# PSUM banks by longest idle time, odd rows' statistics in other steps, edge corrections on GpSimd, and the A sums in two halves

## The chip, the cores and the metric

The kernel runs on one core of a Trainium2 chip. The core has five engines that run side by side and meet only through semaphores: TensorE (PE in the profile) multiplies matrices into PSUM, VectorE (DVE) and ScalarE (ACT) work elementwise and can read PSUM, GpSimd (POOL) works elementwise on SBUF, and SyncE (SP) issues all the DMAs of this kernel. PSUM has eight banks of 128 x 512 fp32 values; SBUF is the working memory. The metric is the device time of one execution in microseconds (us), as a median over runs.

## The reference

A batch of 16 images of 256 channels by 64 x 64 pixels goes through two residual layers, everything in fp32:

```python
x = x + _L0_conv_ref(_gn(x), ...)   # layer 0
x = x + _L1_conv_ref(_gn(x), ...)   # layer 1

# _L0_conv_ref
pooled = x.mean(axis=(2, 3))
angles = jnp.tanh(relu(pooled @ ap_w1.T + ap_b1) @ ap_w2.T + ap_b2) * (math.pi / 4)
w = rotate(base_kernel, angles)                 # bilinear, per image and group
feat = conv3x3(x, w, groups=B * 8)
return feat * sigmoid(relu(pooled @ meta_w1.T + ...) @ meta_w2.T + ...)

# _L1_conv_ref, N = 4096 tokens of 256 channels, 8 heads of 32
q, k = focus(xt @ Wq.T + bq), focus(k)          # relu, / scale, cubed, old norm kept
z = 1.0 / (einsum(q, k.sum(axis=1)) + 1e-06)
out = einsum(q, einsum(k, v)) * z + depthwise5x5(v)
return out @ Wproj.T + bproj
```

`_gn` is a group norm with 32 groups. So every image needs the statistics of its input before the first convolution, and those of the first layer's output before the second layer's products.

## The kernel before

**Stages.** Image b passes through a key loop (16 steps n, `key_step`), a short passage `between`, and an attention loop (17 steps p, `attention_step`). During b's attention loop the 3x3 convolution of image b+1 is run piece by piece, and the input statistics of image b+2 are taken. During b's key loop the rotated weights of b+1 are prepared (`prepare`, a generator that is advanced twice a step). The main loops stand in `tc.manual_schedule()`: every engine gets its instructions in the order in which the Python code records them, and executes them in that order. An instruction that waits holds up all that follow on its engine.

**Convolution of b+1.** A half image u (0, 1) of two strips is convolved in parts. P multiplies odd input rows, A and B use sums of two neighbouring rows that GpSimd makes (`add_rows`, four instructions L384, one for each group j, into `arena`). `PARTS` gives the step at whose end a part is multiplied (`convolve`, four PSUM banks `pc` at once, L405): A in step 2, P in 3, B in 4 for u=0, and 9, 10, 11 for u=1. The next step evicts (`evict`): A first by ScalarE (L432), P by ScalarE (L428) and VectorE (L434), B by VectorE (L430). `SUMS` gives the steps in which the sums are made: 1 and 3, 8 and 10. Four DMAs for each j bring the rows into `arena` (`load_rows`, L371 to L376); for u=0 they are issued in the last key steps (j=3, 2) and just ahead of `between` (j=1, 0). The sums' region overlaps the value buffers `vbuf` 0 to 3 of the key loop.

**Settling.** After P the even rows (s=0) of an output are done, after B the odd ones (s=1). `settle` adds a correction to the first and last column of 8 rows (L443) and takes the statistics of the 512 values (L444). `SETTLES` gives step, (u, s, early q, late q), q running over four outputs. From step 14 on, `norm1` turns these statistics into coefficients: bn_aggr (L190), matmul pm (L196), four small VectorE instructions (L197 to L200), matmul pv (L203), a power on GpSimd (L206), the scaling of the key weights (L531) and matmul pbkv (L538).

**Statistics of b+2.** `more_stats` takes one chunk of 512 columns (L118) and issues the load of the next one into the same buffer `xs` (L109). `STATS` gives the step.

**One attention step.** In this order: ratio (L572, L573, VectorE) and root (L576, GpSimd) for f[p-1]; eviction of output 0; `add_up` (L756: adds py of p-3 to x) and `store` of the result (L762); `turn` (transposes pt, L698) with ScalarE's copy to qT (L703); eviction 1; `cube` of f[p] (GpSimd, L567); query products pq of p+1 (L683) and `query_bias` (VectorE, L557, L558); early settles; a step of `norm1`; evictions 2 and 3 with `turn_back` (transposes po of o, L734, copied by ScalarE, L736) between them; late settles; squares on ScalarE (L564); `attend` (matmuls pn, L715; VectorE zz and o, L717 to L724; GpSimd adds fm to o, L726); `project` (py, L744); sums, loads of value blocks (`load_blocks`, vh, L643, as many as `BLOCKS` says) and of rows; the convolution part; `more_stats`. In step 9 the second half of the depthwise products pd is computed.

**Query weights.** In the key loop `fold_load(b, "q")` loads them, `fold_scale` at n=5 scales them (L531), and `fold_shift` at n=6 multiplies them with the means (pbq, L538) and corrects the bias (L540).

**Banks.** `bank(name)` takes a 128 x 512 tile from a pool of six PSUM buffers with one tag, and the pool chooses the buffer. The remaining two banks hold pkv and pn.

Of the kernel before, what the change touches and what calls it, by code (L numbers as in the profile page):

```python
# [9 lines left out]
F32 = mybir.dt.float32  # L10
# [3 lines left out]
PSUM = bass.MemoryType.PSUM  # L14

P = 128
# [5 lines left out]
CH = 512  # L22
# [2 lines left out]
ROWS = CH // W  # L25


STRIP = 2 * ROWS
PAIRS = ROWS
LATE, LEAD = 3, 2  # L30
# [1 line left out]

PARTS = {2: (0, "A"), 3: (0, "P"), 4: (0, "B"), 9: (1, "A"), 10: (1, "P"), 11: (1, "B")}

SUMS = {1: (0, "A"), 3: (0, "B"), 8: (1, "A"), 10: (1, "B")}

SETTLES = {4: (0, 0, (0, 1), (2, 3)), 5: (0, 1, (0, 1), ()), 6: (0, 1, (2, 3), ()),
           11: (1, 0, (0, 1), (2, 3)), 12: (1, 1, (0, 1), ()), 13: (1, 1, (2, 3), ())}
SECOND, ONES_AT, FOLD_AT = 9, 13, 14

BLOCKS = {1: 2, 2: 4, 3: 3, 4: 4, 5: 1, 6: 1, 7: 1}
PIECES = {5: (0, 5), 6: (5, 10), 7: (10, 16)}
KEY_PIECES = {10: (0, 2), 11: (2, 4), 12: (4, 6), 13: (6, 8)}

STATS = {1: (0,), 2: (1,), 3: (2,), 7: (3,), 8: (4,), 9: (5, 6), 10: (7,)}
RAW = (STRIP + 2) * W
BR, BC = 8, 4
NR, NJ = H // BR, W // BC
# [15 lines left out]
def conv_attention(ctx: ExitStack, tc: tile.TileContext, x, consts, kw, b1, w2, b2, b2r,  # L64
                   wkv, wq, brow, srow, wp, bp, dwb, band, out):
    nc = tc.nc
    B = x.shape[0]

    def pool(name, bufs, **kw):
        return ctx.enter_context(tc.tile_pool(name=name, bufs=bufs, **kw))  # L70
# [7 lines left out]
    sp = pool("stats", 2)  # L78
    wtp = pool("wt", 1)
    dcp = pool("scratch1", 1, space=bass.MemoryType.DRAM)  # L80
    ps = pool("ps", 6, space=PSUM)
    psk = pool("psk", 1, space=PSUM)

    def const(name, shape, src=None):
# [2 lines left out]
            nc.sync.dma_start(t, src)  # L87
        return t

    def bank(name):  # L90
        return ps.tile([P, CH], F32, tag="bank", name=name)

    def halves(a):
        return a.rearrange("(t p) n -> p t n", p=P)
# [90 lines left out]
    def gn_coefs(st, b, which):  # L185


        mv = sp.tile([P, 2, 2], F32, tag="mv", name=f"mv{which}_{b}")
        for t in range(2):
            nc.vector.bn_aggr(mv[:, t, :], st[:, t])  # L190
        yield
        mean, var = mv[:, :, 0], mv[:, :, 1]
        co = sp.tile([P, 5, 2], F32, tag=f"co{which}", name=f"co{which}_{b}")
        a, pooled, d, v, m = (co[:, k, :] for k in range(5))
        pm = bank(f"pm{which}_{b}")[:, 0:2]
        nc.tensor.matmul(pm, lhsT=g8, rhs=mean, start=True, stop=True)  # L196
        nc.vector.tensor_copy(m, pm)  # L197
        nc.vector.tensor_sub(d, mean, m)
        nc.vector.tensor_mul(v, d, d)
        nc.vector.tensor_add(v, v, var)  # L200
        yield
        pv = bank(f"pv{which}_{b}")[:, 0:2]
        nc.tensor.matmul(pv, lhsT=g8, rhs=v, start=True, stop=True)  # L203
        vs = sp.tile([P, 2], F32, tag="vs", name=f"vs{which}_{b}")
        nc.vector.tensor_scalar(vs, pv, EPS_GN, None, ALU.add)
        nc.gpsimd.tensor_tensor(a, vs, mhalf, ALU.pow)  # L206
        yield
        if which == 0:
            nc.vector.tensor_mul(pooled, d, a)
        return a, pooled, m  # L210
# [7 lines left out]
    def prepare(b):  # L218
# [13 lines left out]
                                 start=t == 0, stop=t == 1)  # L232
        h = sp.tile([HID, 2], F32, tag="h", name=f"h_{b}")
        nc.vector.tensor_add(h, ph, b1_t)
        nc.vector.tensor_scalar(h, h, 0.0, None, ALU.max)
        yield
        pa = bank(f"pa_{b}")[:, 0:2 + 2 * HD]
# [10 lines left out]
        nc.vector.tensor_add(z, pa[:, 0:2], b2_t)  # L248
        mod = r_mod
        nc.vector.tensor_add(mod, pmod, b2r_t)  # L250

        nc.scalar.activation(mod, mod, AF.Tanh, scale=0.5)
        cs = sp.tile([P, 3, 2], F32, tag="cs", name=f"cs_{b}")
# [5 lines left out]
        pe = bank(f"pedge_{b}")[:, 0:NH]  # L259
        nc.tensor.matmul(pe, lhsT=sel, rhs=gm.rearrange("p t j -> p (t j)"), start=True, stop=True)  # L260
        nc.vector.tensor_copy(edge, pe)
        state[b]["edge"] = edge
        nc.vector.tensor_scalar(mod, mod, 0.5, 0.5, ALU.mult, ALU.add)
        yield
# [59 lines left out]
        def shifts(t):  # L324


            pb = bank(f"pbias_{b}_{t}")[:, 0:3]
            for j in range(4):
                for dx in range(3):
                    nc.tensor.matmul(pb[ts(j, HD), dx:dx + 1], lhsT=sums[t][:, dx, :], rhs=gm[:, t, j:j + 1],  # L330
                                     start=True, stop=True, tile_position=(0, HD * j))
            nc.vector.tensor_copy(shift[:, t, 0:3], pb)
            nc.vector.tensor_reduce(shift[:, t, 3:4], shift[:, t, 0:3], AX.X, ALU.add)
            nc.vector.tensor_scalar(shift[:, t, 3:4], shift[:, t, 3:4], -1.0, None, ALU.mult)

# [39 lines left out]
            else:  # L375
                nc.sync.dma_start(d, src[:, lo:hi])  # L376

    def add_rows(b, u, part):


        g, s = rows_of(b, u), sums_of(b, part)
        even, odd = (0, 1) if part == "A" else (2, 1)
        for j in range(4):
            nc.gpsimd.tensor_add(s[:, j], g[:, j, odd:odd + STRIP:2], g[:, j, even:even + STRIP - 1:2])  # L384

    def convolve(b, u, part):
# [32 lines left out]
    def evict(b, u, part, q):  # L419

        at, shift = (2 * u + q // 2, q % 2), state[b]["shift"][:, q % 2, 3:4]
        pc = state[b]["pc"][q].rearrange("p (r w) -> p r w", w=W)
        fresh = at not in state[b]["x"]
        if fresh:
            state[b]["x"][at] = xp.tile([P, 2 * CH], F32, tag="x", name=f"x_{b}_{at[0]}_{at[1]}")
        rows = rows_16(b, u, q)
        if part == "P":
            nc.scalar.activation(rows[:, 1], pc, AF.Identity, bias=shift, scale=-1.0)  # L428
        if part == "B":
            nc.vector.tensor_add(rows[:, 1], pc, rows[:, 1])  # L430
        elif fresh:
            nc.scalar.activation(rows[:, 0], pc, AF.Identity, bias=shift)  # L432
        else:
            nc.vector.tensor_add(rows[:, 0], pc, rows[:, 0])  # L434

    def settle(b, u, s, q):

        I, t = 2 * u + q // 2, q % 2
        if u == 0 and q == 0 and s == 0:
            state[b]["st1"] = sp.tile([P, 2, NCH, 6], F32, tag="st1", name=f"st1_{b}")  # L440
        rows, shift = rows_16(b, u, q)[:, s], state[b]["shift"]
        e = rows[:, :, 0:W:W - 1]
        nc.vector.tensor_add(e, e, shift[:, t, 0:3:2].unsqueeze(1).to_broadcast([P, PAIRS, 2]))  # L443
        nc.vector.bn_stats(state[b]["st1"][:, t, 2 * I + s, :], rows)  # L444

    load_kernels(0)
# [57 lines left out]
    for co in range(2):  # L504
        for t in range(2):
            nc.tensor.matmul(pb[:, co:co + 1], lhsT=wp_t[:, t, ts(co, P)], rhs=dwb_t[:, t:t + 1],
                             start=t == 0, stop=t == 1)
    nc.vector.tensor_add(bp_t, bp_t, pb)


    vpad = [dcp.tile([BC, H + 4, NJ, C], F32, tag=f"vpad{n}", name=f"vpad{n}") for n in range(2)]
# [21 lines left out]
    def fold_shift(b, name):  # L533
        w, br = state[b][name]
        n = br.shape[1]
        pb = bank(f"pb{name}_{b}")
        for t in range(2):
            nc.tensor.matmul(pb[:, 0:n], lhsT=state[b]["gn1"][1][:, t:t + 1].to_broadcast([P, P]), rhs=w[:, t, :],  # L538
                             start=t == 0, stop=t == 1)
        nc.vector.tensor_sub(br, br, pb[:, 0:n])  # L540

    def norm1(b):
        a, _, m = yield from gn_coefs(state[b]["st1"], b, 1)
# [48 lines left out]
    def key_bias(b, n, j):  # L592
        _, br = state[b]["kv"]
        f = state[b]["k"][n]
        pm = f["pm"][j]
        relu(f["r"][:, j:j + 1, :], pm[:, 0:C].unsqueeze(1), br[:, 0:C].unsqueeze(1))
        nc.vector.tensor_add(vbuf[n % NV][:, j, 0:HD, :].rearrange("p c h -> p (c h)"), pm[:, C:2 * C], br[:, C:2 * C])

    def key_store(b, n):
        for j in range(2):  # L600
# [47 lines left out]
    def depthwise(b, half, c):  # L648
# [7 lines left out]
        for k in range(4):  # L656
            for j in range(4):
# [6 lines left out]
                )  # L664
        nc.scalar.copy(fm[:, :, c * NH:(c + 4) * NH].rearrange("p T (k h) -> p k T h", k=4),
                       pd.rearrange("p k (T h) -> p k T h", h=NH))


    def blocked(b, m):
# [19 lines left out]
    def query_bias(b, m):  # L689
        f = state[b]["f"][m]  # L690
        relu(f["r"], f["pq"], state[b]["q"][1].unsqueeze(1).to_broadcast([P, 2, C]))

    def turn(b, m):

# [6 lines left out]
    def turned(b, m):  # L701
        qT = op.tile([P, 2, 2, P], F32, tag="qT", name=f"qT_{b}_{m}", bufs=1)
        nc.scalar.copy(qT, state[b]["pt"])  # L703
        state[b]["qT"] = qT

    def attend(b, m):
# [22 lines left out]
    def turn_back(b, m):  # L729

        po = bank(f"po_{b}_{m}").rearrange("p (t j n) -> p t j n", t=2, j=2)
        for j in range(2):
            for t in range(2):
                nc.tensor.transpose(po[:, t, j, :], state[b]["o"][j][:, ts(t, P)], ident)  # L734
        oT = op.tile([P, 2, 2 * P], F32, tag="oT", name=f"oT_{b}_{m}", bufs=1)
        nc.scalar.copy(oT.rearrange("p t (j n) -> p t j n", j=2), po)  # L736
        state[b]["oT"] = oT

    def project(b, m):
# [12 lines left out]
    def add_up(b, m):  # L752
        i, R = divmod(m, 2)
        for co in range(2):
            xt = chunk(b, i, co).rearrange("p (y R n) -> p R y n", y=BR, R=2)[:, R]
            nc.vector.scalar_tensor_tensor(xt, state[b]["py"][:, co], bp_t[:, co:co + 1], xt, ALU.add, ALU.add)  # L756

    def store(b, m):
        I, R = divmod(m, 4)
# [60 lines left out]
    def between(b, more):  # L820
# [25 lines left out]
        values(b, NP - 1)  # L846
        squares(f[0], 1)
        squares(f[1], 0)
        if more and b + 2 < B:
            load_stats(b + 2, 0)  # L850

    def attention_step(b, p, chain):
# [8 lines left out]
        if p - 1 < NP:  # L861
            ratio(f[p - 1], True)
            root(f[p - 1])
        if part:
            evict(b + 1, u, part, 0)
        if p >= 3:
            add_up(b, p - 3)
            store(b, p - 3)
        if p - 1 < NP:
            turn(b, p - 1)  # L870
            turned(b, p - 1)
# [70 lines left out]
    with tc.manual_schedule():  # L942
        fold_load(0, "q")
        made = iter(())
        for b in range(B):
            more = b + 1 < B
            state[b]["f"], state[b]["xq"] = {}, {}
            for n in range(0 if b == 0 else LEAD, NP):
# [13 lines left out]
                    fold_load(b, "q")  # L962
                if n == 5:
                    fold_scale(b, "q")
                if n == 6:
                    fold_shift(b, "q")
                if 7 <= n < 15:
                    load_blocks(b, 2 * n - 14)
# [97 lines left out]
```

## Time and profile before

| | |
|---|---|
| median of three runs | 3659.57 us (3655.64 to 3660.37) |
| profiled execution | 3660.74 us, its span 3659.0 us |
| granted TensorE clock | 0.994 of full speed, mean |
| one image, pbkv to pbkv, from the third on | 221.6 to 222.9 us |
| TENSOR_TENSOR x<-x,shift (L443) | 256 times, mean 263 ns |
| BATCH_NORM_STATS2 st<-x (L444) | 256 times, mean 694 ns |
| BATCH_NORM_STATS2 st<-xs (L118) | 256 times, mean 682 ns, 31.7 us of waits for DMA in 21 places |
| TENSOR_TENSOR arena<-arena (L384, GpSimd) | 244 times, mean 1279 ns |
| TENSOR_TENSOR arena<-arena,consts 128x32 (L316, GpSimd) | 32 times, mean 239 ns |

A line of the profile's waits reads: engine, what it was about to do and its line, then what it waited for, and the total in us, the number of waits and the longest. A line of the timeline reads: start and length in us, engine, line, operation, output<-inputs and their size, number of merged instructions, and in brackets the idle time ahead of it with what ended it. PE is TensorE's matmul, PEld its weight load; SPq is SyncE's issue of DMAs. Durations of matmuls are modelled ends of a pipeline, so neighbouring ones overlap.

### The profile page before, as it was taken

The numbers are of one execution on the slowest core, as the hardware profiler recorded it, in microseconds if no ns is written. First come the engines' busy times: TensorE is split into PE (matmuls) and PEld (weight loads), VectorE is DVE, ScalarE is ACT, GpSimd is POOL, SyncE is SP. The second block draws the span as 40 slices with busy tenths as digits, with TensorE's granted clock in tenths as the row PEclk, the third lists the DMA queues.
The fourth block names the chain that finished last, engine by engine and source line by source line (L and its number), as shares of the span: only waits on it lengthen the run. The fifth ranks groups of instructions, "written<-read, shape, count | busy, mean of one in ns | idle before, by whom it ended". The sixth has DMA issues, their size and how long they took to land. (4 is left out here: it accounts for less than half of the span.)

```text
span 3659.0 us, 109568 instructions
## 1 busy us (share of the span) xinstructions
PE 3425.6 (94%) x43496; PEld 2563.6 (70%) x43496; DVE 2541.2 (69%) x6883; ACT 2034.6 (56%) x6501; POOL 1980.4 (54%) x2298
## 2 busy tenths in 40 slices
PE   2899999999999999999999999999999999999999
PEld 1467777776777767776677777777777677767778
DVE  4667768676686767767677686776866677676656
ACT  2365655647556465654656556475564646546565
POOL 4255555556555465554655555565554655546545
PEclk9899999999999999999999999999999999999999
DMA  4353552625436253452635526354362534525242
GB/s 134 110 180 106 161 159 86 197 87 184 140 115 190 83 189 111 150 172 72 203 106 161 158 87 193 91 185 139 113 191 84 186 114 148 168 77 181 78 145 99
DMA packets 191172, 505.90 MB, mean 138 GB/s; under 512 B 30741, under 2 KB 103959, under 8 KB 178372
## 3 DMA queue, kind: packets, MB, share of 16 engines
q1 hardware_dynamic: 190660, 498.89, 42.8%
q8 instruction: 344, 5.64, 0.6%
q14 instruction: 168, 1.38, 0.1%
HBM read 363.24 MB, written 135.53 MB: 136 GB/s over the span
## 5 line engine op out<-in xcount | busy, mean ns | idle before, releaser
L588 PE MATMUL pk<-wkv,x 128*128 128x512 f32 x2048 | 951.5, 611 | 0.0
L726 POOL TENSOR_TENSOR o<-o,fm 128x256 f32<-128x256 f32 x512 | 364.8, 733 | 918.9 <-DVE o L724 704.7
L588 PEld LDWEIGHTS pk<-wkv,x 128*128 128x128 f32 x2048 | 617.6, 310 | 213.6 <-issue 6.5
L683 PE MATMUL pq<-wq,xq 128*128 128x256 f32 x2048 | 492.2, 383 | 21.7 <-DVE x L434 11.5
L744 PE MATMUL py<-oT,wp 128*128 128x256 f32 x2048 | 505.7, 390 | 0.8 <-ACT oT L736 0.7
L564 ACT ACTIVATE r_k<-rk 128x256 f32<-128x256 f32 x1024 | 416.3, 407 | 152.9 <-POOL rk L567 92.6
L564 ACT ACTIVATE r_q<-rq 128x256 f32<-128x256 f32 x1024 | 413.5, 408 | 138.5 <-POOL rq L567 135.9
L683 PEld LDWEIGHTS pq<-wq,xq 128*128 128x128 f32 x2048 | 369.9, 191 | 72.1 <-DVE x L434 15.3
L736 ACT COPY oT<-po 128x512 f32<-128x512 f32 x256 | 150.1, 586 | 469.5 <-PE po L734 469.1
L744 PEld LDWEIGHTS py<-oT,wp 128*128 128x128 f32 x2048 | 369.2, 189 | 51.4 <-issue 3.6
L567 POOL TENSOR_TENSOR rk<-r_k,rk 128x512 f32<-128x512 f32 x256 | 327.0, 1277 | 96.7 <-ACT r_k L564 94.1
L576 POOL TENSOR_TENSOR s_k<-s_k,phalf 128x2 f32<-128x2 f32 x256 | 176.8, 691 | 356.9 <-DVE s_k L573 345.5
L557 DVE TENSOR_TENSOR pq<-pq,bq 128x512 f32<-128x512 f32 x256 | 177.4, 693 | 272.7 <-PE pq L683 230.6
L608 ACT ACTIVATE rk<-rk,s_k 128x256 f32<-128x256 f32 x512 | 231.4, 499 | 213.7 <-POOL s_k L576 213.7
L567 POOL TENSOR_TENSOR rq<-r_q,rq 128x512 f32<-128x512 f32 x256 | 327.2, 1278 | 0.0
L384 POOL TENSOR_TENSOR arena<-arena 128x512 f32<-128x512 f32 x244 | 303.8, 1279 | 7.1 <-PE pc_0B L405 3.7
L557 DVE TENSOR_TENSOR pk<-pk,bkv 128x256 f32<-128x256 f32 x512 | 218.0, 426 | 121.7 <-PE pk L588 119.9
L703 ACT COPY qT<-pt 128x512 f32<-128x512 f32 x256 | 148.7, 581 | 261.9 <-PE pt L698 260.2
L715 PE MATMUL pn<-kvx,qT 128*128 128x132 f32 x2048 | 274.0, 277 | 0.0
L576 POOL TENSOR_TENSOR s_q<-s_q,phalf 128x2 f32<-128x2 f32 x256 | 179.3, 700 | 144.1 <-DVE s_q L573 140.4
L715 PEld LDWEIGHTS pn<-kvx,qT 128*128 128x128 f32 x2048 | 250.5, 190 | 3.7 <-ACT qT L703 3.1
L658 PE MATMUL pd<-vh,band 107*32 107x128 f32 x8192 | 236.3, 274 | 6.5 <-issue 4.5
(161 smaller groups left out, 5974.1 us busy)
## 6 DMA issues: line engine op xcount, KB each, us to landing
vh<-vpad SPq DMA_DIRECT2D x256, 384.0 KB
vh<-vpad SPq DMA_DIRECT2D x256, 360.0 KB
vpad<-arena SPq DMA_DIRECT2D x512, 128.0 KB
out<-x SPq DMA_DIRECT2D x128, 512.0 KB
xs<-in_x SPq DMA_DIRECT2D x224, 256.0 KB
arena<-in_x SPq DMA_DIRECT2D x248, 144.0 KB
arena<-in_x SPq DMA_DIRECT2D x248, 136.0 KB
xs<-in_x SPq DMA_DIRECT2D x16, 512.0 KB
```

Source lines behind the costliest of these rows:

```text
L384: nc.gpsimd.tensor_add(s[:, j], g[:, j, odd:odd + STRIP:2], g[:, j, even:even + STRIP - 1:2])
L557: nc.vector.tensor_add(pm, pm, bias)
L564: nc.scalar.activation(f["r2"][:, j, :], f["r"][:, j, :], AF.Square, accum_out=f["s"][:, k, j:j + 1])
L567: nc.gpsimd.tensor_mul(f["r"], f["r2"], f["r"])
L576: nc.gpsimd.tensor_tensor(f["s"][:, 3, :], f["s"][:, 2, :], phalf, ALU.pow)
L588: nc.tensor.matmul(pm, lhsT=chunk(b, n // 2, t)[:, T % BC:CH:BC], rhs=w[:, t, :], start=t == 0, stop=t == 1)
L608: nc.scalar.mul(f["r"][:, j, :], f["r"][:, j, :], f["s"][:, 3, j:j + 1])
L658: nc.tensor.matmul(pd[ts(j, HD), k, :].rearrange("p (R m h) -> p R m h", R=4, m=4), lhsT=band_t[:, c + k, :], rhs=vb[:, :, :, j, c + k, :] ...
L683: nc.tensor.matmul(pq[:, j, :], lhsT=xq[:, t, ts(j, P)], rhs=w[:, t, :], start=t == 0, stop=t == 1)
L715: nc.tensor.matmul(pn[:, :, 4 * hh:4 * hh + 4], lhsT=qT[:, hh, j, :], rhs=kvx[:, hh], start=True, stop=True)
L726: nc.gpsimd.tensor_add(o, o, fm[:, 2 * (m % NCH) + j, :])
L744: nc.tensor.matmul(py[:, co].rearrange("p y (J c) -> p J y c", c=BC), lhsT=wp_t[:, t, ts(co, P)], rhs=oT[:, t, :].rearrange("p (J y c) -> ...
```

## The change

`bank` now keeps a list of the free banks in the order in which the code gave them back (`leave`, called after the last reader of a tile has been recorded), and hands out the one that has been in the list longest; each bank is a tag of its own with one buffer. `leave` is recorded for every tile that `bank` gives. The tables `SUMS`, `SETTLES` and `STATS` are changed: the A sums of u=0 are made for j=0, 1 at the end of `between` and for j=2, 3 in step 1; odd rows are settled in steps 8, 9 and 13, 14 instead of 5, 6 and 12, 13; input statistics move among steps 2, 3, 7 and 8. The edge correction moves from VectorE to GpSimd. In `attention_step`, `add_up` and `store` come ahead of eviction 0. `fold_shift` of the query weights moves from n=6 to n=8.

```diff
-SUMS = {1: (0, "A"), 3: (0, "B"), 8: (1, "A"), 10: (1, "B")}
-
-SETTLES = {4: (0, 0, (0, 1), (2, 3)), 5: (0, 1, (0, 1), ()), 6: (0, 1, (2, 3), ()),
-           11: (1, 0, (0, 1), (2, 3)), 12: (1, 1, (0, 1), ()), 13: (1, 1, (2, 3), ())}
+SUMS = {1: (0, "A", (2, 3)), 3: (0, "B", range(4)), 8: (1, "A", range(4)), 10: (1, "B", range(4))}
+
+SETTLES = {4: (0, 0, (0, 1), (2, 3)), 8: (0, 1, (0,), ()), 9: (0, 1, (1, 2), (3,)),
+           11: (1, 0, (0, 1), (2, 3)), 13: (1, 1, (0, 1), ()), 14: (1, 1, (2, 3), ())}
...
-STATS = {1: (0,), 2: (1,), 3: (2,), 7: (3,), 8: (4,), 9: (5, 6), 10: (7,)}
+STATS = {1: (0,), 2: (1, 2), 3: (3,), 7: (4,), 9: (5, 6), 10: (7,)}
...
-    ps = pool("ps", 6, space=PSUM)
+    ps = pool("ps", 1, space=PSUM)
...
+    idle, held = [f"bank{k}" for k in range(BANKS)], {}
+
     def bank(name):
-        return ps.tile([P, CH], F32, tag="bank", name=name)
+        held[name] = idle.pop(0)
+        return ps.tile([P, CH], F32, tag=held[name], name=name)
+
+    def leave(name):
+        idle.append(held.pop(name))
...
-    def add_rows(b, u, part):
+    def add_rows(b, u, part, js=range(4)):
...
-        for j in range(4):
+        for j in js:
             nc.gpsimd.tensor_add(s[:, j], g[:, j, odd:odd + STRIP:2], g[:, j, even:even + STRIP - 1:2])
...
         e = rows[:, :, 0:W:W - 1]
-        nc.vector.tensor_add(e, e, shift[:, t, 0:3:2].unsqueeze(1).to_broadcast([P, PAIRS, 2]))
+        nc.gpsimd.tensor_add(e, e, shift[:, t, 0:3:2].unsqueeze(1).to_broadcast([P, PAIRS, 2]))
         nc.vector.bn_stats(state[b]["st1"][:, t, 2 * I + s, :], rows)
...
         squares(f[1], 0)
+        if more:
+            add_rows(b + 1, 0, "A", (0, 1))
         if more and b + 2 < B:
             load_stats(b + 2, 0)
...
-        if part:
-            evict(b + 1, u, part, 0)
         if p >= 3:
             add_up(b, p - 3)
             store(b, p - 3)
+        if part:
+            evict(b + 1, u, part, 0)
...
-                if n == 6:
+                if n == 8:
                     fold_shift(b, "q")
```

More of the change, by code (lines that the diff above doesn't have):

```diff
@@ L25 @@
 ROWS = CH // W
+BANKS = 6
 STRIP = 2 * ROWS
@@ L197, in gn_coefs @@
         nc.vector.tensor_copy(m, pm)
+        leave(f"pm{which}_{b}")
         nc.vector.tensor_sub(d, mean, m)
@@ L205, in gn_coefs @@
         nc.vector.tensor_scalar(vs, pv, EPS_GN, None, ALU.add)
+        leave(f"pv{which}_{b}")
         nc.gpsimd.tensor_tensor(a, vs, mhalf, ALU.pow)
@@ L234, in prepare @@
         nc.vector.tensor_add(h, ph, b1_t)
+        leave(f"ph_{b}")
         nc.vector.tensor_scalar(h, h, 0.0, None, ALU.max)
@@ L250, in prepare @@
         nc.vector.tensor_add(mod, pmod, b2r_t)
+        leave(f"pa_{b}")
         nc.scalar.activation(mod, mod, AF.Tanh, scale=0.5)
@@ L261, in prepare @@
         nc.vector.tensor_copy(edge, pe)
+        leave(f"pedge_{b}")
         state[b]["edge"] = edge
@@ L332, in shifts @@
             nc.vector.tensor_copy(shift[:, t, 0:3], pb)
+            leave(f"pbias_{b}_{t}")
             nc.vector.tensor_reduce(shift[:, t, 3:4], shift[:, t, 0:3], AX.X, ALU.add)
@@ L434, in evict @@
             nc.vector.tensor_add(rows[:, 0], pc, rows[:, 0])
+        leave(f"pc_{b}_{u}{part}_{q}")
     def settle(b, u, s, q):
@@ L508, in conv_attention @@
     nc.vector.tensor_add(bp_t, bp_t, pb)
+    leave("pb")
     vpad = [dcp.tile([BC, H + 4, NJ, C], F32, tag=f"vpad{n}", name=f"vpad{n}") for n in range(2)]
@@ L540, in fold_shift @@
         nc.vector.tensor_sub(br, br, pb[:, 0:n])
+        leave(f"pb{name}_{b}")
     def norm1(b):
@@ L597, in key_bias @@
         nc.vector.tensor_add(vbuf[n % NV][:, j, 0:HD, :].rearrange("p c h -> p (c h)"), pm[:, C:2 * C], br[:, C:2 * C])
+        leave(f"pk_{b}_{2 * n + j}")
     def key_store(b, n):
@@ L666, in depthwise @@
                        pd.rearrange("p k (T h) -> p k T h", h=NH))
+        leave(f"pd_{b}_{half}_{c}")
     def blocked(b, m):
@@ L691, in query_bias @@
         relu(f["r"], f["pq"], state[b]["q"][1].unsqueeze(1).to_broadcast([P, 2, C]))
+        leave(f"pq_{b}_{m}")
     def turn(b, m):
@@ L703, in turned @@
         nc.scalar.copy(qT, state[b]["pt"])
+        leave(f"pt_{b}_{m}")
         state[b]["qT"] = qT
@@ L736, in turn_back @@
         nc.scalar.copy(oT.rearrange("p t (j n) -> p t j n", j=2), po)
+        leave(f"po_{b}_{m}")
         state[b]["oT"] = oT
@@ L756, in add_up @@
             nc.vector.scalar_tensor_tensor(xt, state[b]["py"][:, co], bp_t[:, co:co + 1], xt, ALU.add, ALU.add)
+        leave(f"py_{b}_{m}")
     def store(b, m):
```

## The prediction

> **What bounds the kernel now.** First the page's table of busy time, then the waits of TensorE.
>
> ```profile
> PE 3425.6 (94%) x43496; PEld 2563.6 (70%) x43496; DVE 2541.2 (69%) x6883; ACT 2034.6 (56%) x6501; POOL 1980.4 (54%) x2298
> ...
> PE po L734 <- POOL o L726: 57.8, 148, 1.1
> PE pbq L538 <- issue: 19.6, 14, 1.4
> PE pv L203 <- DVE co L200: 13.8, 17, 0.9
> PE pq L683 <- DVE x L434: 11.5, 16, 0.7
> PE pq L683 <- ACT qT L703: 10.2, 14, 0.7
> PE pc_0A L405 <- POOL arena L384: 2.7, 15, 0.2
> ```
>
> TensorE (PE) sets the end: only its gaps can be won. The trace's pbkv matmuls, the first of each image's key loop, come every 221.6 to 222.9 us, so I work in one image and write t for us after that image's pbkv (1029.96 in the image shown below), with means over images. A gap shorter than the pipelined matmul hides in its modelled length, so I took each group of matmuls against the same group elsewhere: conv A of the upper half lasts 8.3 us, the equal conv A of the lower half 6.6; pq lasts 1.73 unhindered, po 0.44. In step numbers p of the attention loop, an image loses: 1.65 in step 2 (conv A), 0.93 each in steps 4 and 11 (pq behind pt), 0.96+0.52 in step 6, 0.75+0.52 in step 7, 0.96+0.52 in step 13, 0.13+0.52 in step 14, 1.0 before pv in step 15, 1.56 before pbq in the key loop. Next, the timeline around these places, put together from the answers for single engines.
>
> ```profile
> 1129.39 4.93 POOL L384 TENSOR_TENSOR arena<-arena 128x512 f32<-128x512 f32 x4
> 1134.29 0.69 POOL L576 TENSOR_TENSOR s_q<-s_q,phalf 128x2 f32<-128x2 f32 x1
> 1134.38 6.47 PE L405 MATMUL pc_0A<-arena,wt 32*32 32x512 f32 x186 [0.18 <-POOL arena L384]
> 1129.86 3.21 SPq L643 DMA_DIRECT2D vh<-vpad  x4
> 1136.24 1.27 DVE L118 BATCH_NORM_STATS2 st<-xs 128x6 f32<-128x512 f32 x2
> 1136.95 0.93 SPq L109 DMA_DIRECT2D xs<-in_x  x2
> 1137.76 0.87 DVE L756 SCALAR_TENSOR_TENSOR x<-py,bp,x 128x256 f32<-128x256 f32 x2
> 1141.27 1.89 PE L683 MATMUL pq<-wq,xq 128*128 128x256 f32 x8
> ...
> 1150.95 1.99 PE L683 MATMUL pq<-wq,xq 128*128 128x256 f32 x8 [0.73 <-ACT qT L703]
> 1166.52 0.69 DVE L444 BATCH_NORM_STATS2 st<-x 128x6 f32<-128x512 f32 x1
> 1170.28 1.40 POOL L726 TENSOR_TENSOR o<-o,fm 128x256 f32<-128x256 f32 x2 [7.04 <-PE pq L683]
> 1171.06 0.44 PE L734 MATMUL po<-consts,o 128*128 128x128 f32 x2 [0.80 <-POOL o L726]
> 1173.14 1.18 DVE L443 TENSOR_TENSOR x<-x,shift 128x16 f32<-128x16 f32 x1
> ```
>
> See that conv A waits for the four GpSimd sums; that SP issues the next xs load only after take_stats, behind four vh block loads; that pq(5) waits for qT, the reader of its own bank; and that po waits for o, late because DVE evicts and settles before it.
>
> **The change, part by part.**
>
> *A sums in two halves.* Sums j=0,1 move to the end of `between`. GpSimd is idle there for 6.0 us (t=88.4 to 94.4), and their row loads, j=0 the last, land at 90.2 to 91.6 by the trace's landing events. Two sums (2 x 1.28) end by 94.2, just ahead of s_q(0) at 94.4: cost nothing, up to 0.3 if the cover fails. Sums j=2,3 then end 2.5 us earlier, so conv A no longer waits: -1.65, and take_stats(1) starts 2.4 earlier (t=103.9), since its predecessor zz(1) waited for s_q behind the sums.
>
> *Statistics of xs.* Step 2 takes chunks 1 and 2. Chunk 2 goes into the one buffer that chunk 1 leaves, so DVE stands through a whole load. SP issues it at t=104.6 and 105.2, behind the four vh blocks of 384 KB, issued at 100 to 103.3, whose last landing is at 110.2 (108.3 to 111.7). In all 12 images looked at, the first xs half landed 0.2 to 1.8 us after the last block. I take 0.4 after it (110.6), and the second 0.7 later (111.3; spacing on an idle queue 0.6 to 0.8). Then 0.68 of bn_stats, 0.4 for ratio(2), 0.87 for add_up(0): 113.25. Behind this wait stand ratio, add_up, query_bias and o on DVE. With the new banks pq(4) uses py(0)'s bank and waits for add_up(0); before, it used a bank that ScalarE evicted. So pq(4) starts at 113.3, against 110.3 without the wait and 112.0 before: step 2 and 3 together are +1.3, the gain of the sums more than eaten. Earliest: a load on an idle queue lands 2.7 after issue (107.9), no wait, -1.65. Latest: the second half at 113.9, the worst seen before, +3.9. I take the middle value, since all images show the blocks ahead. The take that leaves step 8, and step 3's, lie beside conv P and cost nothing; chunk 3's load is issued with an empty queue.
>
> *Banks and add_up first.* In steps 4 and 11 pq gets py(p-3)'s bank, released by the add_up that now stands ahead of the first eviction; in step 4 DVE follows pq(4), done at 115.0, with query_bias 1.4, zz and o 1.2 (with gaps 118.0), take_stats(3) 1.3, ratio 0.4 and add_up 0.9: 120.6. TensorE wants the bank after po, pn, py, conv P and pt (0.44+0.9+1.82+3.3+0.45): 122.0. Both stalls go: -0.93 each. Bounds 0 and -0.93.
>
> *Settling of odd rows.* Steps 5, 6, 12, 13 lose two settles each (2 x (0.26+0.69) = 1.9 us of DVE); steps 8, 9, 13, 14 get them. po(4) in step 6 needs o(4) 1.04 earlier, po(5) 1.27 in step 7, and 1.9 less work precedes o(4): both stalls go, -2.75 (bounds 0 and -2.75). Steps 8 and 9 hide theirs beside 7.1 us of depthwise and 6.6 of conv A. Steps 13 to 15 have no convolution for cover: step 13's 1.48 goes, but step 14 gets two settles ahead of bn_aggr. I follow DVE there: bn waits for the edges, which stand behind o(12), s_q and cube on GpSimd (1.4+0.7+1.3); counted from conv B's end, o(11) starts at 5.7, the edges end at 10.0, o(12) starts at 11.9, mv is there at 18.2 and py(12) ends at 17.1. So po(12) loses 0.85 instead of 0.65, pm 1.1, and pv 1.5 instead of 1.0. New 3.45 against old 3.13, and 0.1 for pt: +0.4. Bounds -1.5 (only step 13's gain) and +3.6 (below).
>
> *Edges on GpSimd.* 16 adds of 128x16 per image. L316 (128x32) takes 239 ns, L370 (32x64) 227: 0.24 each, 3.8 us on an engine that is 54% busy; DVE is spared 4.2. In step 4 the edges stand behind the B sums, s_q and cube, so DVE settles some 2 us later than now; the 1.4 us that it idled before conv B's end pays, leaving 0.7, which step 5's lighter load absorbs. Zero; 0.24 x 16 = 3.8 an image if nothing covered it.
>
> The line at 1173.14 shows L443 taking 1.18 us, against 0.17 to 0.18 at its shortest, when GpSimd's cube had started 0.14 earlier. The Trainium skill, "SBUF — State Buffer", section "Who interferes with whom", says why: a VectorE instruction with two SBUF inputs and a GpSimd one that reads SBUF share a read interface, and whoever comes second waits for the whole instruction of the other. It speaks against moving work to GpSimd: each edge add may hold a DVE instruction. By the rule 16 x 0.24 us an image more at worst, 58 us over 15 images or 3671; the sum goes without it, because evictions read PSUM and bn_stats one operand.
>
> *fold_shift from n=6 to 8.* Its gap of 1.56 disappears there, but I price it at zero:
>
> ```profile
> 1290.27 1.10 PE L538 MATMUL pbq<-wq,co 128*128 128x256 f32 x4 [1.40 <-issue]
> ...
> DVE s_k L572 <- ACT r_k L564: 8.3, 6, 2.0
> DVE arena L309 <- POOL rtmp L301: 1.7, 1, 1.7
> ```
>
> The last two lines are all DVE waits between t=36 and 92: none is for TensorE. DVE is full to t=61 and waits for ScalarE thereafter, so key_scale(13) does not come earlier, and values(13) already waits for it (pq in front of it 1.18 too long). What is gained at pbq is waited there. Bound -1.56 if ScalarE follows.
>
> **Sum.** For images 0 to 13: +1.3-0.93-2.75-0.93+0.4 = -2.9, times 14 = -40.7. Image 14 prepares the last one and has no xs to take: -1.65-0.93-2.75-0.93+0.4 = -5.9. The last image has no convolution to run. Together -46.6 on the span of 3659.0 (3660.74 as run; the median shown, 3659.57, is 1.2 lower): 3613 as a median.
>
> **Rivals.**
> (a) The xs load is hidden after all: -5.9 in 15 images, 3571. Against it: blocks landed first in every image. For it: its issue moves 2.4 us forward.
> (b) The pbq gap is truly won: 16 x 1.56 = 25 on top, 3588. Against it: DVE never waits for TensorE there.
> (c) Slower: in steps 13 and 14 DVE stands behind a full GpSimd queue, o pair, s_q and cube (3.4 us), each time, and o of that step follows: +6.8 an image in place of +0.4. That makes -2.9+6.4 = +3.5, 3709. It decides from 3.3 us held in both steps together. For it: no convolution covers; against: po wants o more than 2 us after pt, and the edges of step 13 wait only 0.7.
> (d) No change: GpSimd's edges hold DVE in steps 4 and 11 so that the stalls of steps 6 and 7 stay: -0.2 an image, 3656.
>
> **How the numbers follow.** Forecast 0.56 (its own range 3596 to 3640), (a) 0.13, (b) 0.10, (d) 0.08, (c) 0.13. A measurement here tells 0.2% (7 us) from nothing. Faster: 0.56+0.13+0.10 = 0.79; same 0.08; slower 0.13. The range goes from 3576, which takes in (b) and nearly (a), to 3650 (landings at 113.9, +2.6 x 14 = 36, on 3613); (c), (d) and the end of (a) are left out.
>
> **What would show it.** The profile after should have: DVE st <- DMA xs waiting some 60 to 100 us in total instead of 31.7; pq <- DVE x L756's new line at step 3 with about 3 us of idle; pc_0A as short as pc_1A; no wait of po in steps 6 and 7 (po <- POOL o about half of 57.8); pbq's wait gone and pkv <- ACT rk grown by as much; pm and pv waits grown. I am wrong if pq(4) starts right after pt, if pm or pv stall by over 2 us each, or if the key loop gets shorter.

## The result, and the profile after

The changed kernel takes 3705.99 us as a median of four runs (3696.67 to 3709.21), against 3659.97 for the kernel before on the same chip (four runs, 3655.64 to 3661.78): 1.0129 times as long, with a 95% interval of 1.0116 to 1.0142. The forecast was 3613 us, with a range of 3576 to 3650. The profiled execution is the shortest of the four, 3696.67 us with a span of 3694.5, 35.5 more than before; the some 9 us by which the other runs lie above it are in no trace.

Of the changed kernel, first a line of the page's table of busy time, then lines of the waits (engine, line, what it was about, what it waited for: total us, times, longest). Its lines are numbered higher: pq is L701 instead of L683, add_up L777 instead of L756, po L754 instead of L734.

```profile
PE 3461.2 (94%) x43496; PEld 2591.2 (70%) x43496; DVE 2482.2 (67%) x6627; ACT 2034.2 (55%) x6501; POOL 2032.2 (55%) x2554
...
DVE st L458 <- POOL x L457: 132.0, 92, 6.4
DVE st L125 <- DMA xs<-in_x: 99.9, 35, 7.4
PE pq L701 <- DVE x L777: 47.0, 14, 4.8
PE pv L211 <- DVE s_q L588: 27.4, 15, 1.8
PEld pc_0B L418 <- DVE x L447: 26.7, 17, 12.3
PE pm L203 <- DVE zz L737: 12.8, 15, 0.9
PE po L754 <- POOL o L746: 11.8, 54, 0.3
```

The waits answer to those shown of before as the change meant them to: po waits 11.8 us instead of 57.8, and pq's two waits of 11.5 and 10.2 are gone. In their place stand 47.0 before pq (for add_up), 27.4 before pv, and waits of the B convolution for VectorE. PE's busy time rose from 3425.6 to 3461.2 with the same 43496 matmuls: the same work took longer, and by as much (35.6) as the span grew. The modelled lengths of PE also hide short waits, as those of the B convolution, so not all of it is slower work; the tables below say where it lies.

The next table gives the ledger of one image in us, from the starts of TensorE's groups of matmuls in both traces (means over images 1 to 14, t counted from pbkv).

| place | forecast | measured |
|---|---|---|
| conv A starts | 0 | -0.20 |
| conv A, upper half | -1.65 | -1.01 |
| wait between pt and pq(4), step 3 | +2.95 | +3.28 |
| pq, po, pn right after it | 0 | +1.58 |
| step 4: pq behind pt | -0.93 | -0.99 |
| step 4: conv B | 0 | +0.87 |
| steps 6 and 7: pq and po | -2.75 | -2.74 |
| steps 8 to 10 | 0 | 0 |
| step 11: pq behind pt | -0.93 | -0.98 |
| step 11: conv B | 0 | +0.73 |
| steps 13 to 15: waits up to pv | +0.4 | +0.38 |
| po, pn, py right after pv | 0 | +1.37 |
| sum | -2.9 | +2.3 |

Image 14 takes no statistics and does not wait at pq(4); over images 1 to 13 alone that wait is +3.53. From pbkv to pbkv it is 224.4 us instead of 222.2, 30 us in 14 images; with 5.1 us of start-up (the first pbkv starts at 134.5 instead of 129.5) that makes nearly all of the 35.5 us of the span.

The two places with "right after" are where the same matmuls take longer. The windows view shows why: stretches of 3.41 us around pq(4) of the image whose pbkv is at 1043.88 (the stretch and its length, then busy time of each engine, the granted clock, DMA share and rate).

```profile
1152.07:1155.48 3.41, 1.64 (x34) 0.58 (x22) 0.00 (x0) 2.36 (x4) 0.00 (x0) 1.00 0.43 113
1155.48:1158.90 3.42, 0.42 (x1) 0.45 (x2) 2.30 (x6) 0.08 (x1) 1.28 (x2) 0.51 0.30 99
1158.90:1162.31 3.41, 3.41 (x10) 2.59 (x10) 0.04 (x1) 0.00 (x0) 0.66 (x1) 0.50 0.80 264
1162.31:1165.72 3.41, 3.41 (x36) 2.86 (x50) 3.31 (x9) 2.83 (x10) 0.90 (x2) 0.99 0.32 122
```

In the first stretch TensorE is idle for 1.77 us, in the second for 3.0; the second and the third run at half clock, and in the third ten matmuls take the whole 3.41 us. The trace of before has no such stretch between 230 us and its last microseconds; that of after has 25 drops there, 20 of them of one stretch and five of two. From image 1 on they lie at t = 111 to 116, in 11 images, and at t = 217 to 222, in 12; the other two are in image 0. In the trace of after, with the stretches laid on the recorded changes of the clock, every first stretch at half clock follows one with at least 1.73 us of idle TensorE, and no stretch at full clock follows one with over 1.69: the clock drops when TensorE was idle for half of the 3.41 us before, whatever the number of gaps. (What brings it back is another number, given at the end.)

Next the timeline at the same place (SPq is SyncE's issue of DMAs).

```profile
1146.60 6.53 PE L418 MATMUL pc_0A<-arena,wt 32*32 32x512 f32 x192
1153.06 0.66 PE L717 MATMUL pt<-consts,rq 128*128 128x128 f32 x4
1158.48 3.75 PE L701 MATMUL pq<-wq,xq 128*128 128x256 f32 x8 [4.76 <-DVE x L777]
...
1147.88 1.27 DVE L125 BATCH_NORM_STATS2 st<-xs 128x6 f32<-128x512 f32 x2
1155.93 1.29 DVE L125 BATCH_NORM_STATS2 st<-xs 128x6 f32<-128x512 f32 x2 [6.78 <-DMA xs<-in_x]
1157.46 0.87 DVE L777 SCALAR_TENSOR_TENSOR x<-py,bp,x 128x256 f32<-128x256 f32 x2
...
1143.95 3.20 SPq L660 DMA_DIRECT2D vh<-vpad  x4
1148.59 8.98 SPq L116 DMA_DIRECT2D xs<-in_x  x4
```

Chunk 2 is loaded behind four blocks, VectorE stands 6.78 us for it, add_up(0) comes behind, and pq(4) waits for its bank: the forecast's chain, step by step. Only then does pq take 3.75 us instead of 1.89.

### The profile page after: what moved, and what is told of

It is laid out like the page before. It is cut to its first block, busy times and chain, and to the rows that moved or that the text cites. A ratio compares the mean times of both kernels' runs of the same rounds, so it can differ in the third digit from the quotient of the medians.

```text
span 3694.5 us, 109728 instructions
## 1 busy us (share of the span) xinstructions
PE 3461.2 (94%) x43496; PEld 2591.2 (70%) x43496; DVE 2482.2 (67%) x6627; ACT 2034.2 (55%) x6501; POOL 2032.2 (55%) x2554
## 3 DMA queue, kind: packets, MB, share of 16 engines
q14 instruction: 167, 1.37, 0.1%
## 5 line engine op out<-in xcount | busy, mean ns | idle before, releaser
L701 PE MATMUL pq<-wq,xq 128*128 128x256 f32 x2048 | 509.9, 394 | 47.0 <-DVE x L777 47.0
L765 PE MATMUL py<-oT,wp 128*128 128x256 f32 x2048 | 516.3, 396 | 2.9 <-ACT oT L756 2.5
L701 PEld LDWEIGHTS pq<-wq,xq 128*128 128x128 f32 x2048 | 382.2, 197 | 97.4 <-issue 40.4
L765 PEld LDWEIGHTS py<-oT,wp 128*128 128x128 f32 x2048 | 379.1, 195 | 57.2 <-ACT oT L756 4.3
L756 ACT COPY oT<-po 128x512 f32<-128x512 f32 x256 | 149.8, 585 | 464.6 <-PE po L754 464.0
L735 PE MATMUL pn<-kvx,qT 128*128 128x132 f32 x2048 | 284.8, 284 | 0.0
L735 PEld LDWEIGHTS pn<-kvx,qT 128*128 128x128 f32 x2048 | 260.4, 197 | 4.5 <-ACT qT L722 4.0
L458 DVE BATCH_NORM_STATS2 st<-x 128x6 f32<-128x512 f32 x256 | 165.5, 684 | 132.0 <-POOL x L457 132.0
```

Source lines behind the costliest of these rows:

```text
L701: nc.tensor.matmul(pq[:, j, :], lhsT=xq[:, t, ts(j, P)], rhs=w[:, t, :], start=t == 0, stop=t == 1)
L735: nc.tensor.matmul(pn[:, :, 4 * hh:4 * hh + 4], lhsT=qT[:, hh, j, :], rhs=kvx[:, hh], start=True, stop=True)
L765: nc.tensor.matmul(py[:, co].rearrange("p y (J c) -> p J y c", c=BC), lhsT=wp_t[:, t, ts(co, P)], rhs=oT[:, t, :].rearrange("p (J y c) -> ...
```

## The experiments

All times are medians; each run stood beside runs of the kernel before on the same chip (3658.7 to 3661.9). "Per image" means a mean over images 1 to 14 of its trace.

### Chunk 2 in step 3 again (stats_old)

```diff
-STATS = {1: (0,), 2: (1, 2), 3: (3,), 7: (4,), 9: (5, 6), 10: (7,)}
+STATS = {1: (0,), 2: (1,), 3: (2,), 7: (3,), 8: (4,), 9: (5, 6), 10: (7,)}
```

> The changed kernel with the old table STATS (one chunk of statistics in step 2, chunk 2 in step 3), everything else as changed. Theory (the wait of VectorE for chunk 2 holds add_up(0), whose bank pq(4) needs, and the idle TensorE is then given half the clock): pq(4) starts right after pt in 13 images, so the gap of 3.3 us (mean) and the 1.4 us of slow matmuls behind it both go, about 60 us, 3645; no half-clock stretch near t=115. Rival 1 (the half clock has nothing to do with the gap): only the gap goes, 43 us, 3663, and the half-clock stretches stay. Rival 2 (the bank itself is the trouble: add_up(0) is late anyway, and pq(4) would wait for it without any load): a gap of over 1 us stays before pq(4), 3680 or more.

3647.9 us (ratio to before 0.9968, 0.9952 to 0.9983). pq(4) starts 0.52 after pt instead of 3.77 and takes 1.85; the half clock near t=115 is gone in all images but one, that near t=220 stays. Rival 1 falls with that: slow matmuls and gap go together. Rival 2 falls: add_up(0) without the load is in time, so the new bank alone does not hold pq(4). 14 us of the gain are lost behind step 8, where chunk 4's load is now waited for and the depthwise products of step 9 take 8.17 instead of 7.13: the same kind of wait at another place.

### Edges back on VectorE (edges_dve)

```diff
-        nc.gpsimd.tensor_add(e, e, shift[:, t, 0:3:2].unsqueeze(1)...
+        nc.vector.tensor_add(e, e, shift[:, t, 0:3:2].unsqueeze(1)...
```

> The changed kernel with the edge corrections back on VectorE, everything else as changed. Theory (GpSimd's queue holds the edges, so VectorE's settles and the evictions behind them come late): both B convolutions take 6.5 us again in place of 7.3 to 7.4, 15 x 1.65 = 25 us; in steps 13 to 15 the settles no longer wait 0.46 and 0.78 for edges, the gaps before pm and pv shrink below what brings the half clock near t=220, 13 x 1.4 = 18 us; together about 3660. The start-up of 134.5 us up to the first pbkv tells whether the edges or the banks cost 5 us there: 129 if the edges. Rival (the 4.2 us of VectorE's time that are back are what binds, as the change's sparing would have it): the stalls of po in steps 6, 7 come back, 2.75 an image, and the gaps before pm and pv grow: 3700 or more.

3709.5 us (1.0137, 1.0122 to 1.0153): no faster. My theory of the B convolutions falls, for they take 7.46 with VectorE's edges, against 7.38 and 7.24 with GpSimd's, and the drops near t=220 stay. The start-up part holds: the first pbkv is at 128.5 instead of 134.5. So in the image loop the edges are, if anything, a little better off on GpSimd (0.6 us an image by the medians, which lie only 3.5 us apart), and the start-up pays it back. The 132.0 us that VectorE waits for edges are, on balance, not on TensorE's path.

### Odd rows of the lower half in steps 12 and 13 (settles_late)

```diff
-           11: (1, 0, (0, 1), (2, 3)), 13: (1, 1, (0, 1), ()), 14: (1, 1, (2, 3), ())}
+           11: (1, 0, (0, 1), (2, 3)), 12: (1, 1, (0, 1), ()), 13: (1, 1, (2, 3), ())}
```

> The changed kernel with the odd rows of the lower half settled in steps 12 and 13 again, everything else as changed (the upper half's stay in 8 and 9, edges stay on GpSimd). Theory (two settles ahead of bn_aggr in step 14 make pm and pv late): the gap before pm goes and that before pv halves, -2.0, the half clock near t=220 goes, -1.4, the stall of po in step 13 comes back, +1.48: about -1.9 x 15 = 28 us, 3678. Rival (the edges on GpSimd are what is late, in whatever step): pm and pv wait as long as now and po of step 13 waits as well: 3706 to 3728.

3671.3 us (1.0041, 1.0026 to 1.0056), 35 less than the changed kernel where 28 were expected. Per image: py to pm 1.82 instead of 2.84, pt to pv 1.59 instead of 2.46, pn and py behind pv 0.98 and 1.87 instead of 1.45 and 2.54, and po of step 13 waits again (+1.05). The waits up to pv give 0.8 us of the gain, the clock behind them 1.2, and the drops near t=220 are gone in all images but one.

### TensorE kept busy in the two gaps (fill, fill6)

```diff
+        for r in range({2: 6, 14: 2}.get(m, 0) if b + 1 < B else 0):
+            nc.tensor.matmul(pt[:, r % 2].rearrange("p j n -> p (j n)"), lhsT=wp_t[:, 0, 0:P], rhs=wp_t[:, 1, :],
+                             start=True, stop=True)
         for j in range(2):
             for t in range(2):
                 nc.tensor.transpose(pt[:, t, j, :], state[b]["f"][m]["r"][:, j, ts(t, P)], ident)
```

> The changed kernel with matmuls that nobody reads put ahead of the transposes of pt(2) (12 of 128x256, 2.6 us) and of pt(14) (4, 0.9 us), where TensorE then waits for pq(4)'s bank and for pv; the transposes overwrite them. The waits themselves stay. Theory (TensorE's idle time within a stretch of 3.41 us sets the clock of the next): the half-clock stretches near t=115 and t=220 disappear in nearly all images and with them 1.4 us each, 35 us in all: 3671, although more work is done. Rival (the half clock does not come from the idle time but from elsewhere, or costs nothing since DVE is what is waited for): stretches stay or the time stays, 3706 to 3711.

> As fill, with half the idle matmuls: 6 calls (12 instructions of TensorE, 2.6 us) ahead of pt(2) and 2 (0.9 us) ahead of pt(14), since each call turned out to be two instructions, and fill's 5.2 us delayed pq(4) by 2.3 us itself. Theory (idle time of over half of a 3.41 us stretch halves the clock of the next): pq(4) starts where it does without filling, 114.0, is 1.73 long, and the half-clock stretches near t=115 and t=220 go: -1.5 and -1.25 in 13 images, 36 us: 3670. Rival (nothing is won by the clock, since VectorE is what is waited for): 3700 to 3706.

The lines shown are fill6's; fill has 12 and 4 in place of 6 and 2. With 12 and 4 calls (fill): 3693.8 us (1.0091, 1.0076 to 1.0106). The half-clock stretches go, all but two near t=115, but a call is two instructions, and 5.2 us of filling put off pq(4) by 2.3. With half of it (fill6): 3666.9 us (1.0011, 0.9999 to 1.0022), 39 us less than the changed kernel, with more work for TensorE. pq(4) starts at t = 114.2 as without filling (114.0) and takes 1.84, pn and py behind pv 0.92 and 1.82. In place of 25 drops there are three: two near t=115, one in image 0, none near t=220. The windows around pq(4) in one of its images (pbkv at 1923.82):

```profile
2030.54:2033.95 3.41, 3.41 (x81) 2.10 (x62) 0.00 (x0) 0.69 (x1) 0.00 (x0) 1.00 0.78 223
2033.95:2037.36 3.41, 2.15 (x12) 1.66 (x11) 2.38 (x6) 1.17 (x3) 0.69 (x2) 1.00 0.28 93
2037.36:2040.77 3.41, 3.24 (x21) 3.00 (x22) 1.23 (x3) 1.33 (x4) 1.25 (x2) 1.00 0.84 257
```

The wait is there (TensorE idle for 1.26 us in the second stretch, although filled), and the clock stays at 1.00. This is the cleanest of the tests: pq(4) and pv still wait for what they waited for, TensorE is merely less idle meanwhile, and over 1% of the time came back.

### The banks and add_up alone, on the kernel before (banks_only)

```diff
 def bank(name):
-    return ps.tile([P, CH], F32, tag="bank", name=name)
+    held[name] = idle.pop(0)
+    return ps.tile([P, CH], F32, tag=held[name], name=name)
...
-        if part:
-            evict(b + 1, u, part, 0)
         if p >= 3:
             add_up(b, p - 3)
             store(b, p - 3)
+        if part:
+            evict(b + 1, u, part, 0)
```

> The kernel before with two things of the change alone: the list of banks, and add_up and store ahead of eviction 0. Theory (what pq gains in steps 4 and 11 is waited for again at the B convolution of the same step, whose banks VectorE's evictions of P free no earlier than before): pq is 1.73 in steps 4 and 11 instead of with 0.93 of stall, but both B convolutions take 7.3 instead of 6.5: -0.1 an image, 3655 to 3661. Rival (the prediction's own step: both stalls simply go): -0.93 x 2 x 15 = 28 us, 3631, B convolutions stay at 6.5.

3667.5 us (1.0018, 1.0008 to 1.0028): no gain, and 0.2% longer than before where 3655 to 3661 was expected. (Conv A and the depthwise products of step 9 are also longer, by 0.27 and 0.26 us an image; why was not tested, nor were the two parts tested apart.) Both stalls of pq go (1.73 behind a pt of 0.49), and the B convolutions grow from 6.51 to 7.49 and 7.45 per image. Where this comes from is seen in the timeline of the changed kernel, step 4, with the weight loads of TensorE (PEld):

```profile
1172.05 0.69 DVE L574 TENSOR_TENSOR rq<-pq,eps 128x512 f32<-128x512 f32 x1
1173.28 1.29 DVE L458 BATCH_NORM_STATS2 st<-x 128x6 f32<-128x512 f32 x2 [0.53 <-POOL x L457]
1174.48 1.27 DVE L447 TENSOR_TENSOR x<-pc_0P,x 128x512 f32<-128x512 f32 x2
...
1174.24 7.36 PE L418 MATMUL pc_0B<-arena,wt 32*32 32x512 f32 x192
1175.21 0.56 PEld L418 LDWEIGHTS pc_0B<-arena,wt 32*32 32x32 f32 x33 [0.79 <-DVE x L447]
```

B starts at 1174.24, but a bank it needs still holds P's third output, whose eviction (L447) starts at 1174.48, behind query_bias and two settles; B goes on at 1175.21, when that eviction is done. In the same step of the kernel before, TensorE lost its 0.93 at pq ahead of this, and B met the eviction (L434) in a wait of 0.45 that left its length at 6.51:

```profile
1156.69 0.72 PEld L405 LDWEIGHTS pc_0B<-arena,wt 32*32 32x32 f32 x33 [0.45 <-DVE x L434]
```

### Two blocks moved from step 2 to step 5 (blocks)

```diff
-BLOCKS = {1: 2, 2: 4, 3: 3, 4: 4, 5: 1, 6: 1, 7: 1}
+BLOCKS = {1: 2, 2: 2, 3: 3, 4: 4, 5: 3, 6: 1, 7: 1}
```

> The changed kernel with two of the four vh block loads of step 2 moved on to step 5 (BLOCKS 2: 2, 5: 3); the statistics stay where the change put them. Theory (the load of chunk 2 and TensorE's own code stand behind the blocks): chunk 2 lands two blocks earlier, near t=108.3, before pq(4) needs add_up(0); the gap of 3.3 us goes and the half clock behind it, 1.4; conv A takes 6.46 in every image instead of up to 9.7, mean 7.3: together -5.5 x 13 = 72 us, 3634. Rival (the load is slow whatever lies ahead of it, and conv A waits for its row sums): gap and conv A stay, 3700 or more.

3645.9 us (0.9961, 0.9947 to 0.9975), 60 less than the changed kernel (72 were expected). The wait before pq(4) falls to 1.1, not to nothing, and conv A takes 6.46 in 12 of 15 images where it did in 8; its mean is 6.75 instead of 7.30. So the blocks hold both. The same goes for the other traces with halved A sums: conv A stops in 5 to 7 of 15 images in the eight with four blocks in step 2, in 3 in the three with two. In the changed kernel conv A of the second image stops two instructions from its end:

```profile
471.53 6.51 PE L418 MATMUL pc_0A<-arena,wt 32*32 32x512 f32 x190
480.32 1.00 PE L418 MATMUL pc_0A<-arena,wt 32*32 32x504 f32 x2 [2.28 <-issue]
```

"Issue" means that nothing shown was waited for. The one packet of the instruction queue between 465 and 485 us, 16 KB, starts at 477.74 and takes 1.24, while the blocks' packets are landing (the last at 480.08). That TensorE's code came late behind them fits all this; that the stops go with the blocks is shown, that it is the code is read from the trace only.

### Versions made of the parts (combo1, late, combo2, combo3)

combo1 keeps the banks, add_up first, the halved A sums and the upper half's settles of the change:

```diff
-           11: (1, 0, (0, 1), (2, 3)), 13: (1, 1, (0, 1), ()), 14: (1, 1, (2, 3), ())}
+           11: (1, 0, (0, 1), (2, 3)), 12: (1, 1, (0, 1), ()), 13: (1, 1, (2, 3), ())}
-STATS = {1: (0,), 2: (1, 2), 3: (3,), 7: (4,), 9: (5, 6), 10: (7,)}
+STATS = {1: (0,), 2: (1,), 3: (2,), 6: (3,), 8: (4,), 9: (5, 6), 10: (7,)}
-        nc.gpsimd.tensor_add(e, ...
+        (nc.vector if b == 0 else nc.gpsimd).tensor_add(e, ...
```

> The changed kernel with chunk 2 in step 3, chunks 3 and 4 in steps 6 and 8, the lower half's odd rows settled in 12 and 13 as before, and the edges on VectorE in the start-up only. Theory (each undone part gives what it gave alone, as they lie in different steps): 3706 - 58 (chunk 2's wait) - 14 (no wait for a load in step 8 as stats_old had) - 35 (settles) - 5.5 (start-up) = 3593. Rival (a common engine, VectorE, is short over the whole loop, so that what is freed in one step is lost in the next): 3615 to 3640.

late is combo1 with `4: (0, 0, (), (0, 1, 2, 3))` and `11: (1, 0, (), (0, 1, 2, 3))` in SETTLES, combo2 is combo1 with the BLOCKS above, combo3 has both.

> combo1 with the even rows of steps 4 and 11 settled after all four evictions of P instead of two before evictions 2 and 3 (the same work of VectorE, in another order). Theory (the B convolutions wait for the eviction of P's third output, which stands behind query_bias and two settles): both B convolutions come down from 7.36 and 6.98 to 6.5, -1.3 x 15 = 20 us, 3581. Rival (B waits for its sums on GpSimd or for code, or what is won at B is waited for at po in steps 5 and 12 because o comes as late as before): B stays or po stalls by as much, 3596 to 3605.

> combo1 with two block loads moved from step 2 to step 5. Theory (in every other image TensorE's code comes late behind the blocks, in conv A): conv A 6.5 in place of 7.4 on average, -0.9 x 14 = 13 us, 3588. Rival (the blocks are as much in the way in step 5, of the row loads and of code there): conv A short but other places longer, 3596 to 3605.

> combo1 with both, late settles and moved blocks. Theory: the two add up, -33 us, 3568. Rival (they share VectorE's or the queue's time in step 5): 3580 to 3590.

| | us | ratio to before | conv A | conv B (steps 4, 11) |
|---|---|---|---|---|
| combo1 | 3601.0 | 0.9828 (0.9807 to 0.9848) | 7.42 | 7.37, 6.98 |
| late | 3579.4 | 0.9779 (0.9764 to 0.9793) | 7.18 | 6.65, 6.45 |
| combo2 | 3589.9 | 0.9807 (0.9792 to 0.9821) | 6.64 | 7.51, 7.00 |
| combo3 | 3572.7 | 0.9756 (0.974 to 0.9773) | 6.69 | 6.98, 6.46 |

The theories hold: the undone parts add up (3601 for a forecast of 3593), and a mere change of order on VectorE brings the gain of the banks out, 22 us. The first lines of late's waits at these places, for comparison with the 26.7 above (each total has two long waits of the start-up in it):

```profile
PEld pc_0B L418 <- DVE x L447: 12.9, 2, 12.3
...
PEld pc_0B L418 <- POOL x L457: 5.0, 15, 0.3
```

Only the two of the start-up are left for VectorE; in the images B waits at most 0.3. combo2 and combo3 gain what conv A gains, and lose a little of it: in combo3 the B convolution of step 4 takes 7.2 to 8.4 in six of 15 images (in late in two); what comes late there was not tested. Together late settles and moved blocks save 28 us where 33 were expected. combo3 beats both kernels, by 2.4% and 3.6%.

## Why the prediction was wrong, point by point

Two steps failed. The sum priced each wait of TensorE at its own length and the matmuls behind it at nothing; they ran at half clock, 1.58 + 1.37 us an image. And "Both stalls go: -0.93 each" counted as won what came back at the B convolutions, 1.6 us an image. The other steps were right in kind, some of them mis-sized:

**A sums in two halves.** Right in cause: no image waits for sums any more, and conv A is 6.46 in eight images. It was mis-sized, -1.01 instead of -1.65, because in the other images a stop of 0.8 to 3.3 us appears. The wait for the sums may have covered part of it before; that is not shown. The prediction took the equal convolution of the lower half as proof that 6.6 was free.

**Statistics of xs.** Right: wait, place and chain. pq(4) came at t = 114.0 (mean) where 113.3 was forecast: the last block landed at 111.0 instead of 110.2 (mean of 13 images), the first half of chunk 2 0.6 later and the second 0.6 after that, where 0.4 and 0.7 had been taken. What failed here is the price of the wait: the term for what it does to TensorE's clock is missing, 1.58 us an image, and stats_old and fill6 show it.

**Banks and add_up first.** This step failed outright: "Both stalls go: -0.93 each." They went (-0.99 and -0.98), and 0.87 and 0.73 came back at the B convolution of the same step. The prediction followed VectorE up to the add_up that frees pq's bank, and not to the next thing that TensorE would then need. banks_only shows the loss without any other part of the change, late the remedy.

**Settling of odd rows.** Steps 6 and 7: -2.74 for a forecast of -2.75. Steps 13 to 15: +0.38 for +0.4 as far as the waits go, by waits of 0.4, 1.0 and 2.0 at po(12), pm and pv (forecast 0.85, 1.1 and 1.5) against the 1.5 of step 13. But the gaps of pm and pv lie so close that a stretch of 3.41 us mostly holds over 1.7 us of idle TensorE, and half the clock follows: 1.37 us an image, priced at nothing. The rule "if pm or pv stall by over 2 us each" was too lenient: 1.0 and 2.0 were enough together.

**Edges on GpSimd.** Zero in the sum, as forecast, but not as told: by the medians 0.6 us an image better, some 5 us worse in the start-up, where nothing covers them (first pbkv at 133.8 to 136.2 in the six traces with GpSimd's edges there, 128.2 to 130.7 in the seven with VectorE's). The bound by the Trainium skill, "SBUF — State Buffer", section "Who interferes with whom", 3671, was not needed: edges_dve, which takes the edges off GpSimd again, gives nothing back. (VectorE is held by GpSimd at another place, below, by adds that were there before.)

**fold_shift.** Right: the wait before pbq is gone, and pd starts at t = 85.11 instead of 85.17 (means over images 1 to 14). The waits for ScalarE's rk at pkv grew, as expected: those of its matmuls from 16.2 to 28.4 us, those of its weight loads from 50.6 to 64.2.

**Rivals.** (c) named 3709, nearly the time that came, but not the cause: GpSimd's queue held VectorE 0.46 and 0.78 us for edges in steps 13 and 14 (image with pbkv at 1043.88), far from the 3.3 it needed. (a) and (b) fell by the waits at pq(4) and the unchanged key loop; (d) by the po stalls that went.

What was left out weighs, in 14 images: half clock 2.95 x 14 = 41 us, which fill6 gives back (39); the B convolutions 1.6 x 14 = 22; the stops of conv A 0.64 x 14 = 9; the wait of pq(4) 0.33 x 14 = 5; the start-up 5. That is 82 us, as much as the profiled run lies above what was forecast for its like (35.5 more instead of 46.6 less). So close a fit is partly luck, since smaller terms are left out and some images had other forecasts. The 9 us from there to the median are not explained.

## What to carry to other kernels

A wait on the bounding engine is to be priced with what it does to that engine's clock: steps 13 to 15, whose waits nearly cancel out in the sum, cost half a per cent (1.37 us an image) because two waits lie close together. Where a stall is removed, follow the bounding engine to the next thing it needs and ask whether that is any earlier; if it is not, the gain is only moved. A load that is issued behind big ones should not stand ahead of work that frees a resource, and code may be one of the loads (read from one trace, not shown).

## What the runs showed of the hardware

**The clock.** It is granted in stretches of 3.41 us, at 1.00 or 0.50. Over all thirteen traces, from 230 us on: a stretch at full clock that was followed by half clock had TensorE idle for at least 1.58 us, in 108 of 109 cases (once 1.32); one that was followed by full clock had at most 1.70, in all but two of 12712 (1.77 and 1.99). From half clock it takes much less idle time to stay there: the 113 stretches at half clock that were followed by full clock had at most 0.52 us of idle, the 28 that were followed by another at half clock 0.36 to 3.2. So full clock was lost when about half of a stretch was idle, and came back after a stretch that was nearly full. The Trainium skill, "TensorE: Matmul & The Clock Gate", section "HAM oscillation — how this bites in real kernels", warns of idle gaps of over some 3.4 us; by that rule the 1.0 and 2.0 us before pm and pv would cost nothing beyond themselves. Here they did, and the measurement decides.

**Held VectorE instructions.** On the way from pm to pv of the changed kernel:

```profile
1263.21 0.48 DVE L206 TENSOR_TENSOR co<-mv,co 128x2 f32<-128x2 f32 x1
1263.73 0.65 DVE L207 TENSOR_TENSOR co<-co 128x2 f32<-128x2 f32 x1
1264.41 0.16 DVE L208 TENSOR_TENSOR co<-co,mv 128x2 f32<-128x2 f32 x1
...
1262.95 1.41 POOL L746 TENSOR_TENSOR o<-o,fm 128x256 f32<-128x256 f32 x2 [2.64 <-PE pt L717]
```

While GpSimd adds fm to o (twice 0.7 us, up to 1264.36), VectorE's two-operand instructions on two columns take 0.48 and 0.65 us instead of 0.16. In the kernel before they took 0.16 and 0.62 at this place, so only part of it is new. Of the 2.0 us that pv waits, 0.8 are such holding.
